# Four-layer convolution kernel on one Trainium2 core: the rows of a mixing step made adjacent in DRAM, and two places in a hand-written order moved

## The chip, the cores and the metric

The kernel runs on one NeuronCore of a Trainium2 chip. The metric is the device time of one launch in microseconds, from the first instruction to the last. Before the change it is 2867.51 us, the median of three runs (2860.91 to 2868.28). The profiled execution spans 2862.2 us; every time "in the trace" counts from its start.

## The reference

The input `x` is (4, 64, 256, 256) in float32: 4 images, 64 channels, 256 by 256 points. Four layers follow one another. Layers 0, 2 and 3 are long convolutions, each with its own filters; layer 1 mixes channels in a Haar basis:

```python
# layers 0, 2, 3: k is an outer product of two learned 1-D filters per channel
y = irfft2(rfft2(x, 512x512) * rfft2(k, 512x512))[..., :256, :256]
x = y + x * bias[channel]

# layer 1
f1 = haar2d(x)
acc = 0
for i in range(2):
    f4 = einsum('bchw,oc->bohw', f1 * v[i], conv_w[i])
    acc += sign(f4) * relu(abs(f4) - tau[i])
x = haar2d(acc, inverse=True) + x
```

Because the filter of a convolution is an outer product, the kernel computes it as two triangular Toeplitz products, first along rows and then along columns, with no Fourier transform. A channel needs its own image only in layers 0, 2 and 3; layer 1 needs all 64 channels of one point at once. So the data is laid out by channel in the convolutions and by point in the mixing, and passes through DRAM on the way in and on the way out.

## The kernel before

**Tiles and rounds.** The four images are two groups of two. A round is two channels of one group: a tile of 128 partitions x 8 blocks x 256 values, 1 MB. A group has 32 rounds. A mixing step is 128 points' worth of the transformed image: 64 steps a group, each a tile `ft` of 128 partitions x 2 images x 512 values, 512 KB, with two units, one for each of the two mixing matrices.

**Three phases, written as lists of small closures ("pieces").**

- Phase A, layer 0. For a round: row products `a1ps` and column products `a2ps` (line 307, TensorE), the residual `x*bias + a2ps` (L466, VectorE), the Haar transform along one axis by adds on GpSimd (L355, L357), along the other by a product `a3ps` with a constant matrix (L319), copies out of PSUM by ScalarE (L479), and a store into the DRAM tensor `coef` of its group (L483). Ten pieces a round.
- Phase B, layer 1. For a step: loads of `ft` from `coef`, and of `v` and `tau` (L545, L551); for each unit a mixing product `f` (L590, TensorE), the multiplication by `v` (L605), sign and magnitude (L609, L613, ScalarE), the threshold (L616, L619, VectorE), the sum `gt` (L631, L634, GpSimd); and a store into the DRAM tensor `mixed` (L640). The first two steps are first joined by a few adds on VectorE (`join`, lines 563 to 569), which complete the coarsest levels of the transform.
- Phase C, layers 2 and 3. For a round: a load `g` from `mixed` (L699), the inverse Haar transform on GpSimd (L392) and by a product `c0ps` (L319), then rows and columns of layer 2 (`c1r`, `c1c`) and of layer 3 (`c2r`, `c2c`), all on line 307, the residuals (L759) and the store of `out`. Eighteen pieces a round.

**Order.** The order on every engine is the order in which the pieces are called; no scheduler changes it. `beside(main, side, lead, tail)` deals the pieces of `side` evenly between those of `main`. There are four stages: phase A of group 0 alone; phase A of group 1 as main with phase B of group 0 as side; phase C of group 0 as main with phase B of group 1 as side; phase C of group 1 alone. All transfers are issued by SyncE, in one order.

**Layout in DRAM.** `coef` and `mixed` have 64 blocks of `PAIR` values. A block holds the rows of two neighbouring steps for all 64 channels. Before the change it is ordered [channel parity][round][step of the pair][2 images x 512], so phase A and phase C move 8 KB in a row (both steps of a channel) from one partition, and phase B, which wants one step, takes 4 KB and skips 4 KB, 64 times. One row of 8 KB at the end pads the block to 520 KB. `all_rows` gives the transfers of a round, two of 512 KB, one for each channel parity; `step_of` those of a step, two of 256 KB.

**The start of phase B.** `start` loads three steps; then come three empty pieces, then the joins of both images in one piece, then the first mixing product `mix(0)`, then three pieces a unit.

**The handover between the layers.** The last list of phase A, `a_end`, has four pieces: what remains of the Haar adds of the last round and a store; two Haar products `a3ps` of that round; the last `coef` store. It is dealt by hand into the beginning of phase C, whose first two pieces `c_first` are inverse products of round 0, and whose round list `c` begins with the four row pieces of layer 2.

Of the kernel before, what the change touches and what calls it, by code (L numbers as in the profile page):

```python
# [47 lines left out]
P = 128  # L48
# [3 lines left out]
BLOCKS = N // ROW  # L52
# [13 lines left out]
NB = B // GROUPS  # L66
CI = 4 // NB
M = CI * NB

ROUNDS = C // CI  # L70
STEPS = C
# [2 lines left out]
C_PIECES = 4 * BLOCKS + 2  # L74
W = 2 * N

PAIR = 2 * ROUNDS * 2 * NB * W + 2 * NB * W


IMAGES = (GROUPS, NB, ROUNDS, CI, BLOCKS, ROW, N)  # L80
# [11 lines left out]
def conv_haar_kernel(  # L92
# [10 lines left out]
    def coefficients(name):  # L103
        return dram.tile([CI, STEPS // 2, PAIR], F32, tag=name, name=name)

# [7 lines left out]
    def pool(name, bufs, stack=ctx, **kw):  # L113
        return stack.enter_context(tc.tile_pool(name=name, bufs=bufs, reuse_waits="tile", **kw))
# [185 lines left out]
    def half(r):  # L300
        return slice(r * ROW, (r + 1) * ROW)
# [112 lines left out]

    def all_rows(grp_tile, r, images):

        by_q = images.rearrange("(m q) n k -> q m (n k)", q=2)
        n = 2 * NB * W
        at = [grp_tile.offset + (q * ROUNDS + r) * n for q in range(2)]
        return [(bass.AP(grp_tile.tensor, at[q], [[PAIR, P // 2], [1, n]]), by_q[q]) for q in range(2)]  # L420

    def phase_a():

# [57 lines left out]
        def store(t):  # L481
            for to, f in all_rows(coef[t // ROUNDS], t % ROUNDS, st[t]["f"]):
                nc.sync.dma_start(to, f)  # L483
            st[t].clear()
# [39 lines left out]
    def phase_b(grp):  # L524
# [5 lines left out]
        pieces = []  # L530

        def step_of(ap, s, images):

            n = NB * W
            by_e = images.rearrange("(m e) b w -> e m (b w)", e=CI)
            at = [ap.offset + (e * STEPS // 2 + s // 2) * PAIR + s % 2 * n for e in range(CI)]
            return [(bass.AP(ap.tensor, at[e], [[2 * n, P // CI], [1, n]]), by_e[e]) for e in range(CI)]

        def load(s):
            if s >= STEPS:  # L540
                return
            d = st[s]
            d["f"] = bp.tile([P, NB, W], F32, tag="ft", name=f"ft_{grp}_{s}", bufs=4)
            for rows, f in step_of(coef[grp], s, d["f"]):
                nc.sync.dma_start(f, rows)  # L545
            for name, src in (("v", v), ("tau", taus)):
                t = d[name] = bp.tile([P, 2, W], F32, tag=name, name=f"{name}_{grp}_{s}", bufs=3)

                at = src.offset + s * 4 * W * COPIES
                flat = bass.AP(src.tensor, at, [[2 * W, 2 * COPIES], [0, C // COPIES], [1, 2 * W]])  # L550
                nc.sync.dma_start(t.rearrange("p e w -> p (e w)"), flat)  # L551

        def four(name, at, b):

            tiles = [st[s][name] for s in range(2)]
            tiles.append(bp.tile([P, NB, W], F32, tag="m", name=f"spare_{name}_{grp}_{b}", bufs=3))
            return [t[at, b, bass.ts(h, N)] for t in tiles for h in range(2)]

        def join(image):

            a, b, c, d, t, u = four("f", half(image), image)
            op = nc.vector.tensor_tensor
            op(t, a, b, ALU.add)
            op(b, a, b, ALU.subtract)
            op(u, c, d, ALU.add)
            op(d, c, d, ALU.subtract)
            nc.vector.tensor_copy(c, b)
            op(a, t, u, ALU.add)
            op(b, t, u, ALU.subtract)
# [14 lines left out]
        def mix(u):  # L584
            s, i = divmod(u, 2)
            un[u]["f4"] = bps.tile([P, NB, W], F32, tag="f4", name=f"f4_{grp}_{u}", bufs=1)
            for b in range(NB):
                for r in range(2):
                    q = r ^ b
                    nc.tensor.matmul(  # L590
                        un[u]["f4"][half(q), b, :],
                        mixers[0][half(r), bass.ts(i, C)],
                        st[s]["f"][half(r), b],
                        start=True,
                        stop=True,
                        tile_position=(r * ROW, q * ROW),
                    )
# [40 lines left out]
        def store(s):  # L638
            for to, g in step_of(mixed[grp], s, st[s]["g"]):
                nc.sync.dma_start(to, g)  # L640
            st[s].clear()
# [36 lines left out]
            for s in range(3):  # L678
                load(s)

        pieces += [start] + [lambda: None] * 3 + [lambda: [join(b) for b in range(NB)], lambda: mix(0)]
        for u in range(units + 2):
            for j in range(3):
                pieces.append(lambda u=u, j=j: piece(u, j))
# [2 lines left out]
    def phase_c():  # L687
# [6 lines left out]
        def load(t):  # L694
            if t >= total:
                return
            st[t]["g"] = big("in", f"g_{t}", 3)
            for rows, g in all_rows(mixed[t // ROUNDS], t % ROUNDS, st[t]["g"]):
                nc.sync.dma_start(g, rows)  # L699
# [117 lines left out]
    def beside(main, side, lead, tail, weights=(1,)):  # L817


        weights = [weights[k % len(weights)] for k in range(len(main))]  # L820
        all_of = sum(weights[lead : len(main) - tail])
        done = 0
        for k, p in enumerate(main):
            p()
            want = len(side) * sum(weights[lead : k + 1]) // max(1, all_of)
            for q in side[done:want]:
                q()
            done = max(done, want)
# [3 lines left out]
    cut_a, cut_c = (ROUNDS + 2) * A_PIECES + BLOCKS + 1, (ROUNDS - 2) * C_PIECES  # L832
# [4 lines left out]
    bps = pool("bps", 2, during, space=PSUM)  # L837

    beside(a[cut_a : -2 * A_PIECES], phase_b(0), 2, 0)

    a, head = a[-2 * A_PIECES :], A_PIECES + BLOCKS
# [3 lines left out]
    during.close()  # L845
    bp = pool("b2", 2, during)
    bps = pool("bps2", 2, during, space=PSUM)
    main = c_first + a_end[:1] + c[:BLOCKS] + a_end[1:3] + c[BLOCKS : 2 * BLOCKS + 2] + a_end[3:] + c[2 * BLOCKS + 2 : cut_c]
    beside(main, phase_b(1), len(c_first) + 2 * BLOCKS + 6, 0)
    during.close()  # L850
    beside(c[cut_c:], [], 0, 0)

# [110 lines left out]
```

## Time and profile before

| What | Value |
|---|---|
| median of 3 runs | 2867.51 us |
| PE busy | 2430.4 us, 85% of the span |
| GpSimd busy | 1947.8 us, 68% |
| VectorE busy | 1581.7 us, 55% |
| ScalarE busy | 1429.0 us, 50% |
| moved by DMA | 636.27 MB, mean 222 GB/s |
| `coef` stores | 128 of 512.0 KB |
| `ft` loads | 256 of 256.0 KB |
| `mixed` stores | 256 of 256.0 KB |
| `g` loads | 128 of 512.0 KB |
| first and last mixing product | 465.5 and 2132.3 us |

The stages are read by time: the mixing products begin at 465.5 us, the second pass of them at 1273.3 us, and end at 2132 us. An instruction is named by engine, line and the tiles it writes and reads; `f<-ft,mix` is the mixing product. A wait is put down to the instruction or the transfer that came last, so "PE f L590 <- DMA ft<-coef" means that a mixing product stood until its coefficients had landed. SPq is SyncE issuing a transfer; its time there is that of the issue, not of the transfer.

### The profile page before, as it was taken

How to read it: one execution, taken by the hardware profiler on the slowest of the kernel's cores; microseconds unless marked ns; L12 is line 12 of the kernel's file. 1: busy time of each engine (PE TensorE's matmuls, PEld its weight loads, DVE VectorE, ACT ScalarE, POOL GpSimd, SP SyncE). 2: the span in 40 equal slices, each digit the busy share in tenths (PEclk: the TensorE clock that was granted, in tenths of full speed). 3: DMA queues.
4: the chain of work that ended last, by engine and by line, in shares of the span. 5: the costliest groups of instructions: out<-in, count | busy, mean ns of one | idle time of the engine just before them, and what ended most of it. 6: DMA issues, size and time to landing. Idle time of an engine off the chain costs nothing.

```text
span 2862.2 us, 119602 instructions
## 1 busy us (share of the span) xinstructions
PE 2430.4 (85%) x53276; PEld 1945.7 (68%) x53276; DVE 1581.7 (55%) x1779; ACT 1429.0 (50%) x2361; POOL 1947.8 (68%) x2422
## 2 busy tenths in 40 slices
PE   6999997667677677768888888888889999999999
PEld 5777775444445444547767667676677888888888
DVE  2453335677777777536767767676662333333333
ACT  1222224566566666427666666666663333333332
POOL 2787776877787787748768777776675555655551
PEclk9999998788888788979999999999999999999999
DMA  6668778799899999667888888888875444443432
GB/s 171 230 215 254 239 262 238 241 278 292 274 289 280 275 283 285 215 210 210 259 246 244 261 256 260 258 235 257 238 229 172 155 135 158 131 160 130 161 114 93
DMA packets 223290, 636.27 MB, mean 222 GB/s; under 512 B 39078, under 2 KB 121671, under 8 KB 190264
## 3 DMA queue, kind: packets, MB, share of 16 engines
q1 hardware_dynamic: 222776, 628.62, 71.0%
q8 instruction: 419, 6.86, 1.0%
q14 instruction: 95, 0.78, 0.1%
HBM read 413.12 MB, written 215.35 MB: 220 GB/s over the span
## 4 chain that ended last, share of the span: by engine, by line
PE 41%; DMA 23%; DVE 8%; POOL 4%; issue 4%; ACT 4%; SPq 3%; DVEq 0%; ACTq 0%; POOLq 0%
PE c1c L307 9%; DMA ft<-coef 9%; PE c2r L307 9%; PE c2c L307 7%; PE c1r L307 7%; DMA v<-in_v 4%; PE f L590 4%; PE c0ps L319 3%; DMA mixed<-gt 3%; DMA x<-in_x 2%; DVE a L616 2%; DVE x L605 2%; DMA g<-mixed 1%; DVE m L619 1%; DMA tx<-filt 1%
## 5 line engine op out<-in xcount | busy, mean ns | idle before, releaser
L392 POOL TENSOR_TENSOR i<-i,g 128x16 f32<-128x16 f32 x744 | 394.3, 550 | 486.8 <-ACT g L375 469.3
L590 PE MATMUL f<-ft,mix 64*64 64x512 f32 x2048 | 344.5, 687 | 257.3 <-DMA ft<-coef 189.2
L605 DVE TENSOR_TENSOR x<-f,v 128x1024 f32<-128x1024 f32 x256 | 312.3, 1220 | 254.3 <-PE f L590 137.3
L307 PEld LDWEIGHTS a1ps<-tx,x 64*64 64x64 f32 x8192 | 322.9, 141 | 102.4 <-issue 39.9
L307 PEld LDWEIGHTS c1c<-ty,ch 64*64 64x64 f32 x8192 | 309.1, 135 | 104.8 <-ACT ch L740 57.7
L609 ACT ACTIVATE m<-x 128x1024 f32<-128x1024 f32 x256 | 272.1, 1063 | 213.6 <-DVE x L605 155.7
L307 PEld LDWEIGHTS c2r<-tx,cy 64*64 64x64 f32 x8192 | 306.0, 135 | 101.1 <-ACT ch L740 55.8
L307 PE MATMUL a1ps<-tx,x 64*64 64x192 f32 (+3 forms) x8192 | 350.2, 312 | 23.7 <-issue 9.5
L307 PE MATMUL c1c<-ty,ch 64*64 64x128 f32 (+3 forms) x8192 | 341.7, 304 | 32.4 <-issue 22.2
L307 PEld LDWEIGHTS a2ps<-ty,ay 64*64 64x64 f32 x8192 | 313.5, 141 | 78.5 <-issue 49.5
L307 PE MATMUL c2r<-tx,cy 64*64 64x256 f32 (+3 forms) x8192 | 341.1, 303 | 25.9 <-issue 18.6
L307 PE MATMUL a2ps<-ty,ay 64*64 64x256 f32 (+3 forms) x8192 | 344.6, 312 | 15.3 <-issue 10.7
L616 DVE TENSOR_TENSOR a<-a,tau 128x1024 f32<-128x1024 f32 x256 | 314.0, 1226 | 68.7 <-ACT a L613 65.8
L613 ACT ACTIVATE a<-x 128x1024 f32<-128x1024 f32 x256 | 264.5, 1033 | 174.4 <-DVE m L619 173.9
L740 ACT COPY ch<-c1r 128x512 f32<-128x512 f32 x256 | 137.1, 588 | 402.6 <-PE c1r L307 402.0
L307 PE MATMUL c1r<-tx,z 64*64 64x192 f32 (+3 forms) x8192 | 332.0, 303 | 3.2 <-issue 3.1
L307 PEld LDWEIGHTS c1r<-tx,z 64*64 64x64 f32 x8192 | 306.7, 136 | 40.0 <-issue 22.4
L631 POOL TENSOR_TENSOR gt<-gt,m 128x1024 f32<-128x1024 f32 x128 | 302.8, 2366 | 45.0 <-DVE m L619 41.8
L466 DVE SCALAR_TENSOR_TENSOR x<-x,bias_sb,a2ps 128x512 f32<-128x512 f32 x256 | 179.6, 743 | 271.2 <-PE a2ps L307 261.3
L307 PE MATMUL c2c<-ty,ch 64*64 64x128 f32 (+3 forms) x8192 | 320.3, 299 | 10.3 <-issue 10.2
L619 DVE SCALAR_TENSOR_TENSOR m<-a,m 128x1024 f32<-128x1024 f32 x256 | 313.2, 1223 | 22.0 <-DVE a L616 0.5
L307 PEld LDWEIGHTS c2c<-ty,ch 64*64 64x64 f32 x8192 | 303.5, 135 | 31.3 <-issue 19.0
(71 smaller groups left out, 3194.4 us busy)
## 6 DMA issues: line engine op xcount, KB each, us to landing
coef<-f SPq DMA_DIRECT2D x128, 512.0 KB, 5.8
ft<-coef SPq DMA_DIRECT2D x256, 256.0 KB, 7.5
v<-in_v SPq DMA_DIRECT2D x128, 512.0 KB, 8.5
tau<-taus SPq DMA_DIRECT2D x128, 512.0 KB, 9.8
mixed<-gt SPq DMA_DIRECT2D x256, 256.0 KB, 8.5
g<-mixed SPq DMA_DIRECT2D x128, 512.0 KB, 7.7
x<-in_x SPq DMA_DIRECT2D x63, 1024.0 KB, 6.2
out<-o SPq DMA_DIRECT2D x63, 1024.0 KB, 5.3
```

Of the source, the lines that this page charges most:

```text
L307: nc.tensor.matmul(ps[r][half(c), j % 2, k * ROW :], data[half(r), c, k, bass.ts(j, ROW)], t(r, c)[:, : N - k * ROW], start=k == 0, stop=k ...
L319: nc.tensor.matmul(ps[r][half(c)].rearrange("p h k -> p (h k)"), matrix[half(r)], pairs(r, c).rearrange("p h k -> p (h k)"), start=True, s ...
L392: engine.tensor_tensor(to, s, d, op)
L466: nc.vector.scalar_tensor_tensor(to, old, bias_sb[:, c : c + 1], ps, ALU.mult, ALU.add)
L590: nc.tensor.matmul(un[u]["f4"][half(q), b, :], mixers[0][half(r), bass.ts(i, C)], st[s]["f"][half(r), b], start=True, stop=True, tile_posi ...
L605: nc.vector.tensor_tensor(un[u]["x"], un[u]["f4"], both(u, "v"), ALU.mult)
L609: nc.scalar.activation(un[u]["m"], un[u]["x"], AF.Sign)
L613: nc.scalar.activation(un[u]["a"], un[u]["x"], AF.Abs)
L616: nc.vector.tensor_tensor(un[u]["a"], un[u]["a"], both(u, "tau"), ALU.subtract)
L619: nc.vector.scalar_tensor_tensor(un[u]["m"], un[u]["a"], 0.0, un[u]["m"], ALU.max, ALU.mult)
L631: nc.gpsimd.tensor_tensor(st[s]["g"], st[s]["g"], m, ALU.add)
L740: later(lambda y=y, ps=ps: nc.scalar.copy(y, ps))
```

## The change

Three edits. The first swaps two levels of the layout of `coef` and `mixed`: a block is now ordered [step of the pair][channel parity][round][2 images x 512], so that the 64 rows of a step lie in one run of 256 KB, for the loads of `ft` and the stores of `mixed`. For the rounds the two halves of a partition's data now go to two places, so `all_rows` gives four transfers of 256 KB with rows of 4 KB. The block's padding is one row again, now 4 KB.

The second puts ten empty pieces in place of three ahead of the joins and the first mixing product, so that more of the main list is issued before them. The third moves the last two Haar products of layer 0 and the last `coef` store behind all row and column products of layer 2's first round; the mixing of group 1 still begins two pieces behind that store.

```diff
-PAIR = 2 * ROUNDS * 2 * NB * W + 2 * NB * W
+PAIR = 2 * 2 * ROUNDS * NB * W + NB * W
...
     def all_rows(grp_tile, r, images):
-        by_q = images.rearrange("(m q) n k -> q m (n k)", q=2)
-        n = 2 * NB * W
-        at = [grp_tile.offset + (q * ROUNDS + r) * n for q in range(2)]
-        return [(bass.AP(grp_tile.tensor, at[q], [[PAIR, P // 2], [1, n]]), by_q[q]) for q in range(2)]
+        parts = images.rearrange("(m q) (h n) k -> h q m (n k)", q=2, h=2)
+        n = NB * W
+        pairs = []
+        for h in range(2):
+            for q in range(2):
+                at = grp_tile.offset + ((h * 2 + q) * ROUNDS + r) * n
+                pairs.append((bass.AP(grp_tile.tensor, at, [[PAIR, P // 2], [1, n]]), parts[h][q]))
+        return pairs
...
-            at = [ap.offset + (e * STEPS // 2 + s // 2) * PAIR + s % 2 * n for e in range(CI)]
-            return [(bass.AP(ap.tensor, at[e], [[2 * n, P // CI], [1, n]]), by_e[e]) for e in range(CI)]
+            at = [ap.offset + (e * STEPS // 2 + s // 2) * PAIR + s % 2 * P // CI * n for e in range(CI)]
+            return [(bass.AP(ap.tensor, at[e], [[n, P // CI], [1, n]]), by_e[e]) for e in range(CI)]
...
-        pieces += [start] + [lambda: None] * 3 + [lambda: [join(b) for b in range(NB)], lambda: mix(0)]
+        pieces += [start] + [lambda: None] * 10 + [lambda: [join(b) for b in range(NB)], lambda: mix(0)]
...
-    main = c_first + a_end[:1] + c[:BLOCKS] + a_end[1:3] + c[BLOCKS : 2 * BLOCKS + 2] + a_end[3:] + c[2 * BLOCKS + 2 : cut_c]
-    beside(main, phase_b(1), len(c_first) + 2 * BLOCKS + 6, 0)
+    mid, ends = 2 * BLOCKS + 2, 3 * BLOCKS + 2
+    main = c_first + a_end[:1] + c[:BLOCKS] + c[mid:ends] + a_end[1:] + c[BLOCKS:mid] + c[ends:cut_c]
+    beside(main, phase_b(1), len(c_first) + len(a_end) + 2 * BLOCKS, 0)
```

## The prediction

> **What bounds the kernel now.** I read the table of stretches first, because the four stages have different limits and the shares over the whole span mix them. Columns: length, busy us of each engine, granted TensorE clock, busy share of the 16 DMA engines, GB/s.
>
> ```profile
> 0.00:450.00 450.00, 402.71 (x9324) 331.45 (x9328) 171.13 (x252) 116.96 (x211) 316.24 (x531) 0.98 0.71 229
> 500.00:1190.00 690.00, 483.93 (x7866) 320.45 (x7863) 501.94 (x470) 425.33 (x570) 542.94 (x599) 0.84 0.90 276
> 1300.00:2130.00 830.00, 716.33 (x15405) 579.94 (x15400) 583.40 (x591) 552.14 (x884) 617.55 (x633) 0.95 0.84 247
> 2200.00:2860.00 660.00, 651.05 (x17088) 577.99 (x17080) 225.64 (x322) 242.32 (x531) 340.79 (x476) 1.00 0.42 138
> ```
>
> Layer 0 alone (row 1) and layers 2 and 3 alone (row 4) are TensorE's: PE is busy 402.71 of 450 and 651.05 of 660 us. In row 2, layer 0 of group 1 with the mixing of group 0 beside it, PE is busy only 484 of 690 us and DMA 0.90 of the time: the feed sets the pace. Row 3 lies between (PE 0.86, DMA 0.84). Then the table of who waited for whom, PE's rows (us in total, times, longest):
>
> ```profile
> PE f L590 <- DMA ft<-coef: 189.2, 54, 7.2
> PE f L590 <- DVE ft L569: 25.1, 4, 14.7
> ```
>
> The first is the mixing product waiting for its coefficients to land; asked by stretch, 155.1 us of it fall in row 2 and 34.1 in row 3. The second, the joins, is two holes, one at the start of each mixing pass. They stand in the order of time (start, length, instruction, idle time before):
>
> ```profile
> 465.49 1.13 PE L590 MATMUL f<-ft,mix 64*64 64x512 f32 x3 [9.00 <-DVE ft L569]
> 1273.34 1.12 PE L590 MATMUL f<-ft,mix 64*64 64x512 f32 x3 [14.70 <-DVE ft L569]
> ```
>
> PE stood still for 9.00 and 14.70 us. The clock around the first hole:
>
> ```profile
> 460.00:465.00 5.00, 0.00 (x0) 0.00 (x0) 1.35 (x4) 0.00 (x0) 3.11 (x12) 0.57 1.03 229
> 465.00:470.00 5.00, 3.79 (x22) 1.14 (x23) 3.00 (x9) 0.00 (x0) 0.00 (x0) 0.50 1.04 218
> 470.00:475.00 5.00, 5.00 (x63) 4.28 (x64) 2.20 (x2) 3.21 (x4) 0.00 (x0) 0.57 1.03 266
> ```
>
> So a hole costs more than itself: PE works at half clock until 475. DMA was saturated all through (1.03): the hole idles PE, not the feed. For the handover between the layers, SyncE's queue in order of time:
>
> ```profile
> 1241.49 3.19 SPq L699 DMA_DIRECT2D g<-mixed  x4
> 1244.73 3.06 SPq L149 DMA_DIRECT2D tx<-filt  x4
> 1247.84 1.51 SPq L149 DMA_DIRECT2D ty<-filt  x2
> 1250.19 3.44 SPq L149 DMA_DIRECT2D tx<-filt  x4
> 1253.72 1.68 SPq L149 DMA_DIRECT2D ty<-filt  x2
> 1255.50 1.18 SPq L483 DMA_DIRECT2D coef<-f  x2
> 1256.73 0.72 SPq L677 DMA_DIRECT2D mix<-in_pack  x1
> 1259.92 1.12 SPq L545 DMA_DIRECT2D ft<-coef  x2
> ```
>
> The last coefficients of layer 0 go out at 1255.50 behind 12 filter loads, and the first mixing load waits for their landing (1259.92).
>
> **What the Trainium skill says.** (1) "TensorE: Matmul & The Clock Gate", Part 1: PE's clock falls to half after an idle window of about 3.4 us and needs about as much work to return. The trace agrees on the fall (0.57, then 0.50) and shows a longer return (full again by 475 to 480). (2) "DMA: Bandwidth & Descriptors", Rules for kernel authors: two transfers to disjoint halves of the partitions share the same 16 engines, so splitting gives no bandwidth. No run here shows it by itself; I use it as: four transfers in place of two move their bytes in the same time. (3) Same page, Latency and other measured facts: a row pitch of a large power of two in DRAM is slow and 4 KiB of padding restores it. Here the pitch of a pair is 520 KB before, 516 KB after, both padded; the trace agrees for 520, since coef packets of 8192 B took 309 ns in the median, like the contiguous x packets.
>
> **The change, part by part.** *Rows of a step.* A step's loads (ft, 2 x 256 KB) and stores (mixed, 2 x 256 KB) become contiguous in DRAM; a round's coef stores and g loads become 4 x 256 KB in 4 KB rows instead of 2 x 512 KB in 8 KB rows. What it can give: the packet records of row 2, put to their transfers in queue order, give 206 ns for an ft packet and 200 ns for a mixed one, mean; the commonest and lowest value of both is 159. If adjacency removed the whole excess: (47+41) ns x 128 packets / 16 engines = 0.70 us a step, 45 us over 64 steps. If the excess is other traffic (v and tau, 228 and 237 ns, run beside them) it gives nothing. An isolated ft packet already takes 159 ns, so I take a sixth, 8 us, ends 0 and 45. What it costs: packets, 309 ns against 2 x 159, nothing; issues, 128 more for coef and 128 for g, 256 x about 0.55 us (coef 1.18/2, g 3.19/4). Alone, layer 0 hides them: SyncE waited there 65.0 us in 150 to 440 for x buffers (released by the residual); the end hides them too (PE 99% busy). In the mixed stages 28 and 30 rounds have 2 more each: 116 x 0.55 = 64 us of SyncE's time, and behind them in the queue stand the ft loads that PE waits for. The program has eight completion semaphores, so each transfer waits for the landing of the eighth before it, and SyncE mostly waits for landings there: added issue time then shortens that wait. I take 0 in the forecast, ends 0 and 64.
>
> *Later first products.* The joins and the first mixing product stand seven side pieces later. By the listing of the order, half a round of row products and half a round of column products of layer 0 go ahead of it at the first start: 350.2/64/2 + 344.6/64/2 = 5.4 us into the 9.0 us hole. It falls to about 3.6 us and the clock may not fall; 8.8 us of PE work at half clock lost 4.4. Together 9.8 us of PE time at most. The mixing itself still begins when ft lands, and this stage is fed by DMA, so I take half, 5 us, ends 0 and 10. The joins wait on DVE; behind them stand layer 0's residuals, which now come first.
>
> *Handover.* Column products of layer 2's round 0 go ahead of the last Haar products. They need the copies of c1r, which ACT ended at 1250.0, so PE waits about 2.6 us where the Haar products stood (1248.53). Columns end near 1255, Haar products near 1258, their copies near 1260. SyncE stands at the coef store till then, and behind it now come 4 g loads, 12 filter loads and only then the mixing loads: 20 issues x 0.55 = 11 us, so ft goes out near 1271.6 instead of 1259.92, and mixing starts near 1285 instead of 1273.3, 12 us later. Ahead of it PE does 3/4 of a round's c1r and c2r and one inverse product more: 3/4 x 332.0/64 + 3/4 x 341.1/64 + 1.3 = 9.2 us. If PE's work is all that counts, 12 - 9 = +3 us less a little half clock; if the mixing chain sets the stage, +12; if PE is kept warm and the mixing catches up, -4. I take +2.
>
> Sum: -8 + 0 - 5 + 2 = -11 us, **2856 us**.
>
> **The rivals.** *A, forecast, 2856*: chance 0.40. *B, slower*: the mixing of group 1 starts 12 us late and two thirds of that stay (+8), an eighth of the 64 us of issues delays ft (+8), the first start gives 3: +13, 2880. For it: PE's 189.2 us of waiting are for exactly what queues behind the new issues. Against: row 3 has PE at 0.86, so late mixing can be caught up. Chance 0.30. *C, no change*: adjacency gives nothing because a lone packet is at its floor, the start gives 4, the handover takes 4: 2867. Against it: three independent parts must cancel. Chance 0.20. *D, adjacency pays*: five eighths of the 45 us, 28, with -5 and +2: -31, 2836. For it: row 2 is bound by DMA, so an engine's saving counts in full; against: the median packet. Chance 0.10.
>
> **How the numbers follow.** 0.3% is 8.6 us. Faster: D and nine tenths of A, 0.46. Within: C and the rest of A, 0.24. Slower: B, 0.30. The range reaches from a little under D to a little over B, 2832 to 2884: outside it lie the full 45 us on one side and the full issue cost on the other.
>
> **What would show it.** In the waits of PE, the line from the joins should fall from 25.1 us; at the first start the hole should be about 3.6 us and the clock stay up. PE's wait for ft should fall below 155 us in row 2 if adjacency pays, and rise if the issues count. At the handover SyncE should show the coef store ahead of the filter loads and ft some 12 us later. If row 2's length in the changed kernel moves by more than 15 us either way, my reading of the packets is wrong; if the stages alone move, the reading that they hide the issues is wrong.

## The result, and the profile after

The changed kernel takes **2848.14 us** (median of 4 runs, 2843.19 to 2851.65), against 2864.96 us for the kernel before (median of 4 runs, 2860.91 to 2868.28): a ratio of **0.9941, interval 0.9919 to 0.9963**, or 17 us less. The forecast was 2856. Its sum was near, but two of its terms were far off in opposite directions, as the experiments show.

First the same four stretches as before, in the changed kernel (length, busy us of PE, PEld, DVE, ACT and POOL, granted TensorE clock, DMA share, GB/s):

```profile
0.00:450.00 450.00, 401.70 (x9246) 329.34 (x9246) 170.11 (x251) 116.95 (x211) 314.03 (x524) 0.98 0.72 227
500.00:1190.00 690.00, 486.50 (x7968) 315.68 (x7964) 500.26 (x468) 426.72 (x572) 545.54 (x601) 0.86 0.91 279
1300.00:2130.00 830.00, 715.09 (x15409) 572.05 (x15405) 585.61 (x591) 556.90 (x894) 615.11 (x632) 0.95 0.84 250
2200.00:2850.00 650.00, 643.41 (x16976) 574.46 (x16966) 224.91 (x321) 239.19 (x524) 339.78 (x473) 1.00 0.43 138
```

Row by row they look alike, because the windows are fixed and the work moved through them. DMA moved 279 GB/s in row 2 where it moved 276, and 250 in row 3 where it moved 247, at about the same busy share: some 1% more work in the same time. Sizes come out better between marks that belong to the work: the first and last mixing product of each group, and the end.

| us | first pass of mixing | between the passes | second pass | last mixing product to end |
|---|---|---|---|---|
| before | 710.6 | 97.2 | 859.0 | 729.9 |
| after | 701.2 | 107.4 | 850.1 | 722.5 |

Three parts are shorter, by 9.4, 8.9 and 7.4 us, and one is 10.2 us longer: the handover between the layers. The part ahead of the first mixing product (465.5 us before, 468.7 after) is 3.2 us longer. Each row of the table is one profiled execution. The table of PE's waits in the changed kernel (total us, times, longest):

```profile
PE f L595 <- DMA ft<-coef: 180.5, 58, 6.6
PE f L595 <- DVE x L610: 38.5, 30, 3.6
...
PE f L595 <- DVE ft L574: 9.8, 3, 8.5
```

The joins' line (DVE ft) fell from 25.1 to 9.8 us, and its 8.5 us belong to the second start alone. The wait for `ft` fell from 189.2 to 180.5; asked for 500 to 1190 us, from 155.1 to 128.8. In the second pass it rose instead (1300 to 2120 us, before and after):

```profile
PE f L590 <- DMA ft<-coef: 31.3, 12, 6.1
PE f L595 <- DMA ft<-coef: 49.6, 14, 6.6
```

while PE's waits for "issue", in which it waits for nothing that the profile shows, fell there from 53.3 to 34.1 us in sum.

The first start, in PE's order of time and as a table of stretches:

```profile
464.75 0.51 PE L307 MATMUL a1ps<-tx,x 64*64 64x128 f32 x13 [3.39 <-issue]
...
465.14 3.82 PE L307 MATMUL a2ps<-ty,ay 64*64 64x256 f32 x60
468.73 0.80 PE L595 MATMUL f<-ft,mix 64*64 64x512 f32 x1
```

```profile
460.00:465.00 5.00, 1.61 (x45) 1.24 (x41) 0.48 (x1) 0.60 (x2) 4.68 (x9) 1.00 1.03 241
465.00:470.00 5.00, 5.00 (x86) 3.96 (x77) 3.90 (x11) 1.07 (x2) 1.34 (x7) 0.66 1.04 247
470.00:475.00 5.00, 4.42 (x81) 3.26 (x83) 4.16 (x7) 1.85 (x2) 0.00 (x0) 1.00 1.04 261
```

The hole of 9.00 us in front of the mixing product is gone. Column products of layer 0 (`a2ps`) run right up to it. A hole of 3.39 us is left, but it stands ahead of row products (`a1ps`), and nothing that the profile shows ends it. The clock still dips, in one stretch (0.66) where it lay at 0.50 to 0.57 in three. At the handover, SyncE's queue, and the first column product of layer 2 and the first mixing product of group 1:

```profile
1248.64 2.40 SPq L488 DMA_DIRECT2D coef<-f  x4
1251.14 2.46 SPq L704 DMA_DIRECT2D g<-mixed  x4
1253.65 2.50 SPq L149 DMA_DIRECT2D tx<-filt  x4
1256.20 1.23 SPq L149 DMA_DIRECT2D ty<-filt  x2
1257.47 3.32 SPq L149 DMA_DIRECT2D tx<-filt  x4
1260.89 1.18 SPq L149 DMA_DIRECT2D ty<-filt  x2
1262.11 0.58 SPq L682 DMA_DIRECT2D mix<-in_pack  x1
1262.73 1.11 SPq L550 DMA_DIRECT2D ft<-coef  x2
```

```profile
1241.17 5.32 PE L307 MATMUL c1c<-ty,ch 64*64 64x256 f32 x122 [1.74 <-ACT ch L745]
...
1277.30 1.98 PE L595 MATMUL f<-ft,mix 64*64 64x512 f32 x6 [8.54 <-DVE ft L574]
```

The `coef` store now stands ahead of `g` and the filters, and the mixing loads behind them, as forecast. Counted from the first inverse product of phase C (1238.8 us before, 1231.2 after), the first mixing product went from +34.5 to +46.1 us: 11.6 us later.

### The profile page after: what moved, and what is told of

It reads as the page before. It is cut to its first block, busy times and chain, and to the rows that moved or that the text cites. A ratio compares the mean times of both kernels' runs of the same rounds, so it can differ in the third digit from the quotient of the medians.

```text
span 2849.9 us, 120142 instructions
## 1 busy us (share of the span) xinstructions
PE 2429.2 (85%) x53276; PEld 1931.0 (68%) x53276; DVE 1582.2 (56%) x1779; ACT 1427.8 (50%) x2361; POOL 1947.6 (68%) x2422
## 4 chain that ended last, share of the span: by engine, by line
PE 40%; DMA 23%; DVE 9%; ACT 5%; POOL 4%; issue 3%; SPq 3%; DVEq 0%; ACTq 0%; POOLq 0%
PE c1c L307 8%; PE c2r L307 8%; PE c2c L307 7%; PE c1r L307 6%; DMA ft<-coef 6%; DMA v<-in_v 4%; DMA tau<-taus 4%; PE f L595 3%; PE c0ps L319 3%; DMA x<-in_x 3%; DVE a L621 2%; DMA mixed<-gt 2%; DVE x L610 2%; DMA g<-mixed 2%; PE a2ps L307 1%
## 5 line engine op out<-in xcount | busy, mean ns | idle before, releaser
L595 PE MATMUL f<-ft,mix 64*64 64x512 f32 x2048 | 341.3, 687 | 262.2 <-DMA ft<-coef 180.5
L610 DVE TENSOR_TENSOR x<-f,v 128x1024 f32<-128x1024 f32 x256 | 312.0, 1219 | 267.0 <-PE f L595 140.4
L307 PEld LDWEIGHTS c1c<-ty,ch 64*64 64x64 f32 x8192 | 300.9, 133 | 90.2 <-ACT ch L745 53.1
L307 PE MATMUL c1c<-ty,ch 64*64 64x192 f32 (+3 forms) x8192 | 330.3, 299 | 22.8 <-issue 12.7
L307 PE MATMUL c1r<-tx,z 64*64 64x64 f32 (+3 forms) x8192 | 329.9, 302 | 12.5 <-ACT g L375 6.8
L307 PE MATMUL c2c<-ty,ch 64*64 64x192 f32 (+3 forms) x8192 | 319.3, 298 | 9.2 <-issue 9.2
```

The lines of the kernel that those rows point to most:

```text
L307: nc.tensor.matmul(ps[r][half(c), j % 2, k * ROW :], data[half(r), c, k, bass.ts(j, ROW)], t(r, c)[:, : N - k * ROW], start=k == 0, stop=k ...
L595: nc.tensor.matmul(un[u]["f4"][half(q), b, :], mixers[0][half(r), bass.ts(i, C)], st[s]["f"][half(r), b], start=True, stop=True, tile_posi ...
L610: nc.vector.tensor_tensor(un[u]["x"], un[u]["f4"], both(u, "v"), ALU.mult)
```

## The experiments

My theory after the result was that adjacency had paid more than 8 us and the handover had cost more than 2. The rivals: that only the shorter rows and smaller transfers of the rounds matter; that the later first products make the gain; that the moved Haar products are harmless. Every combination of the three edits was timed (layout, late = ten empty pieces, order = moved Haar products and store), and then parts of the layout edit. Each ratio is to runs of the kernel before from the same session; layout with order ran on another chip than the other experiments.

| layout | late | order | ratio to before | interval |
|---|---|---|---|---|
| – | yes | – | 0.9996 | 0.9975 to 1.0017 |
| – | – | yes | 1.0065 | 1.0050 to 1.0081 |
| – | yes | yes | 1.0025 | 1.0009 to 1.0042 |
| yes | – | – | 0.9926 | 0.9907 to 0.9945 |
| yes | yes | – | **0.9878** | 0.9857 to 0.9899 |
| yes | – | yes | 0.9965 | 0.9948 to 0.9982 |
| yes | yes | yes | 0.9941 | 0.9919 to 0.9963 |

Each edit can be read four times, with the others absent or present. Layout: -0.0074, -0.0118 (with late), -0.0100 (with order), -0.0084 (with both), mean -0.0094, or **-27 us** of 2867. Late: -0.0004, -0.0048, -0.0040, -0.0024, mean -0.0029, **-8 us**. Order: +0.0065, +0.0029, +0.0039, +0.0063, mean +0.0049, **+14 us**. With the intervals above, each of these means is uncertain by about 4 us (half-widths of some 0.0019 for seven ratios, added as squares, divided by 4). An interaction is what two edits do together beyond the sum of both. Averaged over the third edit, none is resolved: the largest is 0.0014, uncertain by 0.0025. All three together lie 0.0060 off a plain sum, uncertain by 0.0051, so single readings of one edit differ a little more than the intervals explain; nothing is built on that here.

### The layout alone

The first part of the change's diff, nothing else.

> The adjacent rows alone, with three empty pieces and the old handover. Feed theory (the forecast's): shorter transfers in the mixing stages give 8 us, so 0.997 of before, and both mixing passes are about 4 us shorter each. Order theory: the whole gain comes from the two moved places, so adjacency gives nothing and its 116 extra issues in the mixing stages cost 0 to 10 us, 1.000 to 1.004. All-adjacency: 15 us or more, 0.995 or lower.

Measured: 0.9926 (0.9907 to 0.9945), median 2848.35 us. Most of the gain is here, and nearly three times the forecast's 8 us; it clears the mark written for adjacency as the only cause (0.995).

### The later first products alone

```diff
-        pieces += [start] + [lambda: None] * 3 + [lambda: [join(b) for b in range(NB)], lambda: mix(0)]
+        pieces += [start] + [lambda: None] * 10 + [lambda: [join(b) for b in range(NB)], lambda: mix(0)]
```

> Ten empty pieces in place of three, nothing else. Feed theory: 5 us, 0.998; TensorE's hole ahead of the first mixing product shrinks from 9.0 to about 3.6 us at the first start and by about 5 us at the second. Order theory: 10 us or more, 0.9965 or lower, since the half clock goes as well. All-adjacency: 1.000.

Measured: 0.9996 (0.9975 to 1.0017). The wait for the joins is gone from the top of PE's waits, but without the other edits no gain can be told from nothing. The holes, at the first and at the second start:

```profile
466.41 0.49 PE L307 MATMUL a1ps<-tx,x 64*64 64x128 f32 x8 [3.27 <-issue]
1272.00 1.98 PE L590 MATMUL f<-ft,mix 64*64 64x512 f32 x6 [5.63 <-DVE ft L569]
```

At the first start the rest of the hole stands ahead of row products, as in the changed kernel. At the second it fell from 14.70 to 5.63 us, 9 us where I expected 5.

### The moved Haar products alone

```diff
-    main = c_first + a_end[:1] + c[:BLOCKS] + a_end[1:3] + c[BLOCKS : 2 * BLOCKS + 2] + a_end[3:] + c[2 * BLOCKS + 2 : cut_c]
+    main = c_first + a_end[:1] + c[:BLOCKS] + c[mid:ends] + a_end[1:] + c[BLOCKS:mid] + c[ends:cut_c]
```

(with the `beside` line of the change)

> The moved Haar products and coef store alone. All theories that hold to the forecast's handover: the mixing of group 1 starts 12 us later and 2 to 8 us of that stay, 1.001 to 1.003; with only three empty pieces TensorE has less to do meanwhile. Order theory: this too gains some us, 0.998.

Measured: 1.0065 (1.0050 to 1.0081): alone, this edit makes the kernel 19 us slower, twice the most that I had allowed (1.003). PE's waits say where:

```profile
PE f L590 <- DMA ft<-coef: 197.0, 57, 8.2
PE f L590 <- DVE ft L569: 35.2, 4, 23.5
```

The longest hole in front of the joins grew from 14.7 to 23.5 us, and the wait for `ft` did not shrink in return.

### Both moved places in the old layout

The two edits above together.

> Both moved places in the old layout: the changed kernel without its first edit. Feed theory: 3 us faster than before, 0.999. Order theory: the whole gain, 0.994. All-adjacency: 1.000.

Measured: 1.0025 (1.0009 to 1.0042), above all three expectations. Against it the changed kernel (0.9941) shows what the layout gives beside them: 0.0084, 24 us.

### Layout and moved products, without the ten pieces

> The adjacency edit and the moved Haar products and coefficient store together, with the old three empty pieces ahead of the first mixing product: the one combination of the three edits not yet measured. If the costs of the moved products and of the early start add to the gain of the layout (0.9926 times 1.0065), 0.999, within 0.997 to 1.001. If the layout leaves room for the late mixing to be caught up, 0.993 to 0.996.

Measured: 0.9965 (0.9948 to 0.9982), between the two expectations (just below the interval of the first). Its handover shows what the ten pieces are for, in PE's order of time:

```profile
1247.34 2.16 PE L319 MATMUL c0ps<-ci,inverse_sb 64*64 64x512 f32 x14
1273.94 1.98 PE L595 MATMUL f<-ft,mix 64*64 64x512 f32 x6 [24.44 <-DMA tau<-taus]
```

PE stands for 24.44 us, with the first mixing product at the head of its queue. In the changed kernel a part of this time is filled with products of layer 2, and 8.54 us are left in front of the mixing.

### Layout and late products, without the moved ones

The changed kernel with the old `main` and `beside` lines.

> The changed kernel without the moved Haar products. If the three edits add: 0.9926 x 0.9996, so 0.992, 5 us below the changed kernel. If the ten empty pieces need the moved products to be of use, or the other way round: 0.994, no better than the changed kernel.

Measured: **0.9878 (0.9857 to 0.9899)**, median 2836.65 us (2830.30 to 2841.18). This beats both kernels and both expectations; its interval lies below that of the whole change. The third edit thus costs 0.0063, 18 us, where it stands. Its second start:

```profile
1246.32 1.04 PE L319 MATMUL c0ps<-ci,inverse_sb 64*64 64x512 f32 x8
1252.99 1.98 PE L595 MATMUL f<-ft,mix 64*64 64x512 f32 x6 [5.63 <-DVE ft L574]
```

The first inverse product stands at 1214.2 us in this run, so mixing begins 38.8 us after it, against 46.1 in the changed kernel.

### The Haar products and the store moved less far

```diff
-    main = c_first + a_end[:1] + c[:BLOCKS] + c[mid:ends] + a_end[1:] + c[BLOCKS:mid] + c[ends:cut_c]
+    main = c_first + a_end[:1] + c[:BLOCKS] + a_end[1:] + c[mid:ends] + c[BLOCKS:mid] + c[ends:cut_c]
```

against the changed kernel: the store ahead of the columns of layer 2's first round, the mixing still begun where the change begins it.

> The changed kernel, with layer 0's last Haar products and coefficient store put ahead of the columns of layer 2's first round instead of behind them. If the late store is what the third edit costs, this is no slower than the layout with the ten empty pieces and the old handover (0.9878 of the kernel before): 0.985 to 0.989, the coefficient store is issued about 9 us earlier after the first inverse product than in the changed kernel, and the second mixing pass begins 5 to 10 us earlier. If any disturbance of the old handover costs about 18 us, whatever the position of the store, it is at 0.994 like the changed kernel.

Measured: 0.9919 (0.9888 to 0.9949), between the two. The interval takes in the changed kernel's 0.9941; it overlaps the interval of the old handover (to 0.9899), but leaves out its 0.9878. So it decides for neither expectation. In the same view of SyncE:

```profile
1234.93 2.77 SPq L488 DMA_DIRECT2D coef<-f  x4
...
1250.44 1.11 SPq L550 DMA_DIRECT2D ft<-coef  x2
```

Against the first inverse product (1221.2 us) the store goes out at +13.7 us instead of +17.4, which is 3.7 us and not the 9 I expected, and `ft` at +29.2 instead of +31.5. The mixing begins at +43.7 instead of +46.1, 2.4 us earlier and not 5 to 10. The `ft` loads gain less than the store, because they still stand behind `g` and the filters. With the old order, in the run just above, the store goes out at +16.8 (no earlier than in the changed kernel) but `ft` at +20.0. By these traces it isn't the store's own time that delays the mixing, but what stands between it and the mixing loads. No run puts the mixing loads ahead of `g` and the filters, so this is read from the queue and not tested alone.

### Twenty empty pieces

```diff
-        pieces += [start] + [lambda: None] * 10 + [lambda: [join(b) for b in range(NB)], lambda: mix(0)]
+        pieces += [start] + [lambda: None] * 20 + [lambda: [join(b) for b in range(NB)], lambda: mix(0)]
```

on the layout and the old handover.

> The changed kernel with the old handover (0.9878) and twenty empty pieces in place of ten ahead of the first mixing product. If ten already close the hole in front of the first mixing product, ten more only move the mixing back: 0.987 to 0.992, no wait for the joins is left at the first start. If the gain of the later start is an even further fall of the waits, it goes on: 0.983 to 0.986.

Measured: 0.9926 (0.9898 to 0.9953), slower than with ten pieces (0.9878) by 0.0048, uncertain by 0.0034. The joins' wait is gone from the top of the waits; the mixing starts at 483.8 instead of 463.9 us, and the time between the passes grows to 116.9 us from 99.9. Ten pieces had already taken what there was.

### Short rows and four transfers, without adjacency

```diff
-        at = [grp_tile.offset + (q * ROUNDS + r) * n for q in range(2)]
...
+                at = grp_tile.offset + ((q * ROUNDS + r) * 2 + h) * n
...
```

for `h` and `q` in 2 x 2 with `n` halved, in the old layout: a round's `coef` stores and `g` loads are four of 256 KB with 4 KB rows, with 256 more issues, as in the change, but a step's rows stay 4 KB apart.

> The old layout, but a round's store and load each as four transfers of 4 KB rows: the first edit's extra issues and shorter rows without its adjacency. Adjacency theory: no gain, 1.000 to 1.004. Packet theory (rows of 4 KB leave the DMA engines sooner to whoever waits behind them, such as the instruction fetches, which pass through the same engines): the whole gain, 0.990 to 0.995, with TensorE's waits for issue in the stretch from 1300 to 2130 down from 53 us to about 40.

Measured: 0.9974 (0.9959 to 0.9989). So 256 more issues together with shorter transfers cost nothing; the split is even a little faster, 7 us, between the two expectations. What the issues cost by themselves, this run doesn't separate. PE's waits for "issue" from 1300 to 2130 us, which should have fallen from 53 to about 40 us if shorter rows made way for instruction fetches, are at 54.1: in that stage this theory fails. The Trainium skill, "DMA: Bandwidth & Descriptors", Rules for kernel authors, advises to join many small transfers into a large one, and says that under 64 KB one pays mostly overhead. 256 KB is well above that, and here the smaller transfers gained 0.26%. The rest of the layout's gain, 0.9926 against 0.9974 or 14 us (uncertain by 7), is adjacency.

### Adjacency in one tensor only

`coef` in the new layout and `mixed` in the old one, and the reverse:

```diff
+PAIRS = {True: 2 * 2 * ROUNDS * NB * W + NB * W, False: 2 * ROUNDS * 2 * NB * W + 2 * NB * W}
+ADJ_COEF, ADJ_MIXED = True, False
...
```

(`False, True` in the second run; `all_rows` and `step_of` take the layout of their tensor)

> Adjacent rows in coef alone (the stores of layer 0, the loads of the mixing steps). Adjacency theory with faster ft loads: half the gain or more, 0.993 to 0.996. Packet theory with the g loads as the place: little, 0.998 to 1.001.

> Adjacent rows in mixed alone (the stores of the mixing steps, the loads g of layer 2). Since the comparison of the stages puts the gain behind 1277 us and none ahead of it: nearly the whole gain, 0.992 to 0.995, by either theory. If the forecast's place (ft) were right: 0.998 to 1.001.

Measured: `coef` 0.9948 (0.9926 to 0.9970), `mixed` 0.9982 (0.9966 to 0.9997). Their product is 0.9930, the layout's 0.9926: the two add, and `coef` is the greater part. Nearly the whole gain, as I had expected of `mixed` from the stages of single executions, did not come; 0.9982 lies where I had put it if the forecast's place, the `ft` loads, were right. Each of these runs also has the split of its own tensor's transfers in it.

### The block's padding

```diff
-PAIR = 2 * 2 * ROUNDS * NB * W + NB * W
+PAIR = 2 * 2 * ROUNDS * NB * W + 2 * NB * W
```

on the layout alone: blocks of 520 KB instead of 516.

> The adjacency edit alone, but with the block padded to 520 KB as before the change instead of 516 KB. If the adjacency of a step's rows makes the gain, nothing changes against the edit alone: 0.991 to 0.995. If the new pitch of the blocks makes it, only the gain of the shorter rows is left: 0.996 to 0.999.

Measured: 0.9924 (0.9896 to 0.9952), the same as 0.9926. The pitch of the blocks is not the cause.

## Why the prediction was right, and where it was wrong

| term | forecast | measured (mean of four readings) |
|---|---|---|
| adjacency of rows, with its transfers | -8 | -27 |
| more issues | 0 | not measured apart: with the shorter transfers, -7 |
| later first products | -5 | -8 |
| handover | +2 | +14 |
| sum | -11 | -21; the change itself: -17 |

The total held because two wrong terms, 19 us too little gain and 12 us too little cost, cancelled for the most part; no argument of the prediction made them cancel, so that is luck.

**Adjacency was undersized, and by another way than the one priced.** The step that failed is "I take a sixth, 8 us". It priced adjacency by shorter packets, took a lone packet at its 159 ns floor as a sign that little could be won, and counted only the step's transfers in the stage bound by DMA. In that stage the packets did not get shorter. The split and the layout alone have the same transfers and differ in adjacency; their queue in 500 to 1190 us (packets, MB, share of the 16 engines) is, the split first:

```profile
q1 hardware_dynamic: 60332, 188.83, 89.6%
q1 hardware_dynamic: 60415, 189.15, 90.4%
```

That is 0.2% more bytes for 0.9% more time of the DMA engines; by the packet records a 4 KB packet took 213 ns in the mean without adjacency and 215 with it. Only in the second pass (1300 to 2120 us) are these packets shorter: 217 to 223 ns in the eight kernels with adjacent `mixed`, 228 to 233 in the six others.

The profiled executions, one each, put the gain in three places. They lie up to 12 us from the median of their kernel (the split 2876.75 against 2864.74, `mixed` only 2855.84 against 2866.08), so a difference of a few us between two of them carries little; what counts below is where all kernels of one kind lie on one side. (a) PE's wait for `ft` in 500 to 1190 us is 144.5 to 163.9 us in the six kernels with the old `coef` layout (before, late, order, late with order, split, `mixed` only), and 128.8 to 149.3 in six with the new one (layout, `coef` only, padding, layout with late, with order, with both). The means are 157.7 and 139.9; the two sets overlap, but in each of the four pairs with and without the layout the wait is shorter with it. (With the store first it is 124.4, with twenty pieces 142.9.) But the first pass itself became only some 5 us shorter by the four pairs with and without the layout: other waits took some of the rest, as "DVE x L610" in the waits above (38.5 us, against 13.7 for the same line before). (b) The second pass takes 857.7 to 863.2 us in the kernel before and the three of the table with the old layout, and 849.8 to 854.8 in the four with the new one: 9 us in the mean. (In the split it took 871.3; adjacent `coef` or `mixed` alone gave 853.6 and 851.5.) PE's waits for "issue" there are 44.4 to 54.1 us in the five kernels without adjacency, and 30.5 to 44.5 in the nine with it in one tensor or both. That is the stage where I thought late work could be caught up. (c) From the last mixing product to the end, where nothing mixes, PE's row is, before and after:

```profile
2132.30:2862.20 729.90, 711.15 (x18592) 630.31 (x18584) 249.77 (x353) 269.90 (x588) 381.58 (x526) 0.99 0.43 141
```

```profile
2127.40:2849.90 722.50, 708.66 (x18592) 630.50 (x18584) 250.86 (x355) 269.68 (x587) 381.44 (x526) 0.99 0.44 144
```

The same 18592 products, 7.4 us less. It goes with the `g` loads: with two of 512 KB a round this stretch takes 728.9 to 731.8 us (before, late, order, both, `coef` only), with four of 256 KB 719.9 to 725.7 (the other nine kernels, the split without adjacency among them at 724.5). So this part belongs to the split, not to adjacency, and is as large as the split's whole gain. In the prediction's words, a stage alone moved, but towards less time: that more issues stay hidden there stands, but the shorter time I had not thought of. PE's waits for "issue" ahead of c2r, in which it waits for nothing that the profile shows, fell there from 5.8 to 1.2 us.

What adjacency changes in the DRAM or in the DMA engines to make the passes shorter isn't settled. The time from issue to landing doesn't tell it: in 500 to 1190 us,

```profile
mixed<-gt SPq DMA_DIRECT2D x126, 256.0 KB, 8.6
ft<-coef SPq DMA_DIRECT2D x118, 256.0 KB, 8.3
```

before,

```profile
mixed<-gt SPq DMA_DIRECT2D x128, 256.0 KB, 6.8
ft<-coef SPq DMA_DIRECT2D x118, 256.0 KB, 6.3
```

after, but in the split without adjacency

```profile
mixed<-gt SPq DMA_DIRECT2D x124, 256.0 KB, 7.6
ft<-coef SPq DMA_DIRECT2D x118, 256.0 KB, 6.0
```

so an `ft` load lands sooner by the split alone, while the wait of PE for it stayed long there (160.7 us). Row 2's length moved by 9.4 us, less than the 15 I had named as the bound of my packet reading; the reading passes that test, but the packets above do not bear out what it assumed.

**More issues: not contradicted.** 256 more, with shorter transfers, made nothing slower (0.9974), and the same bytes took the same time of the engines in 500 to 1190 us (188.83 MB at 89.6% in the split, 189.56 MB at 89.7% before). The rule that the prediction took for this from the Trainium skill ("DMA: Bandwidth & Descriptors", Rules for kernel authors) speaks of halves of the partitions; the split halves rows. That the shorter waits for landings take the issues up, as I argued, was not shown by itself, and PE's wait for `ft` did grow in the second pass, from 31.3 us before to 36.9 in the split. The price of 0.55 us an issue was too low for its own lines (1.18 / 2 = 0.59 and 3.19 / 4 = 0.80).

**Later first products: right in size**, with -8 against -5. The hole of 3.39 us has the forecast's size (3.6) but not its place or cause: it was to be what is left of the wait for the joins, and it stands ahead of row products instead, so the agreement does not confirm the sum. The clock did fall, but for a shorter time. This edit gave -1 us alone and -14 with the layout, a little more apart than the intervals allow (0.0044, uncertain by 0.0035); with the moved products in place the difference has the other sign (-0.0040 without the layout, -0.0024 with it), so I draw nothing from it.

**Handover: right mechanism, wrong price.** The order in SyncE's queue, the 11.6 us (12 forecast) and PE's wait for the copies of c1r (1.74 us, 2.6 forecast) came out. What failed is the step from 12 us late to +2, which credited 9.2 us of PE work done earlier. The time between the passes is 107.3 to 109.0 us in the four kernels with the moved products and 96.0 to 99.9 in those four without: 10 us. The second pass isn't shorter for it: in the four pairs it changed by +0.3, +2.9, +3.1 and -5.5 us, nothing in the mean. PE at 0.86 of row 3 looked like room to catch up, but the work done early bought no time that can be seen. "If the mixing chain sets the stage, +12" was the case to choose. Of the 14 us, 10 are thus placed; the other 4 are within the uncertainty.

The rivals: D had the size of the adjacency (28 us), B the cost of the handover (+8, too little still), and C's cancelling of parts took place, at another level.

## What to carry to other kernels

When an edit has several parts that can pull in opposite directions, time their combinations: here one of them without the last part (0.9878) beats the whole (0.9941), and the whole looked like a plain success. Here a start of the mixing 12 us later cost 14 us (uncertain by 4), whatever TensorE had done ahead of it: price a later start of a chain in full, until a run shows that the work done early counts. Rows that one transfer takes, put in one run of DRAM, were worth some 14 us here; look for such a gain in every stage, not only where DMA is fullest.

## What the runs showed of the hardware that was not expected

- Four transfers of 256 KB in 4 KB rows in place of two of 512 KB in 8 KB rows, same bytes: 0.9974 (0.9959 to 0.9989), and by the profiled executions the gain lies in a stretch where DMA is busy 0.43 of the time and PE 0.97 (711.15 of 729.90 us). Why PE runs with fewer unexplained waits there is open.
- Rows of 4 KB that lie end to end, rather than every second one, gave another 14 us (uncertain by 7), though in row 2 the bytes moved per busy time of the DMA engines hardly changed: both kernels move 307 GB/s for a full busy share (276 / 0.90 and 279 / 0.91). In the second pass 4 KB packets took 217 to 223 ns with adjacent `mixed` and 228 to 233 without.
- A block pitch of 516 or 520 KB makes no difference (0.9926 and 0.9924). The Trainium skill, "DMA: Bandwidth & Descriptors", Latency and other measured facts, asks that a row pitch of a large power of two be padded by a few KB; both pitches here are so padded (512 KB and 4 or 8), and no run has one that isn't, so its advice is not tested.
- Before, after a hole of 9.00 us, the clock still lay at 0.57 in the stretch from 470 to 475 us; after a hole of 3.39 us it lay at 0.66 from 465 to 470 and at 1.00 in the next stretch.
